# Unit-matrix products on TensorE for one operand turn and five weight parts, with a new order of head and tail

## The chip, the cores and the metric

The kernel runs on one core of a Trainium2 chip. The core has a matrix engine (TensorE, PE in the profile; its weight loads are PEld), a vector engine (VectorE, DVE), a scalar engine (ScalarE, ACT), a general engine (GpSimd, POOL) and SyncE (SP), whose queue issues nearly all transfers. The engines run their own instruction streams in order and wait for one another by semaphores. TensorE writes its results into banks of PSUM; DVE and ACT read them from there. The metric is the device time of one execution in microseconds; the median of five runs is used. All times are microseconds unless marked otherwise.

## The reference

There are 128 graphs of 128 nodes with 512 features (`x`, 128x128x512, float32) and a weighted adjacency (`adj`, 128x128x128). Two layers run one after the other for each graph:

```python
# layer 0
h = max(layernorm(x), 0)
H = (adj != 0); w = adj[:, 0, :]              # hyperedge weights: first row
S = H diag(1/colsum(H)) H^T;  Dinv = 1/(H w)
r = relu(Dinv * (S @ (h @ W1^T)) + b1)         # 512 -> 1024
r = layernorm(r) * gamma + beta
y = Dinv * (S @ (r @ W2^T)) + b2               # 1024 -> 512
x = x + (y + h)
# layer 1
h = max(layernorm(x), 0)
agg = (adj @ h) / max(rowsum(adj), eps)
x = x + relu([h, agg] @ W^T)                   # 1024 -> 512
```

Results are wanted in float32.

## The kernel before, in words

**Products in three parts.** A float32 product runs on TensorE in the faster format fp32r by splitting both operands into three parts: a high part `h` (ACT, a scaled copy), a low part `l` (DVE or POOL, the difference) and a third part `d` (DVE). `product` (L392 to L408) puts `h` by `h` and `l` by `l` into one PSUM bank (`rm`, `gm`, `bm`, `am` by the product's name; L401) and `d` by `d` into a second (`rd`, `gd`, `bd`, `ad`; L406). ACT and DVE then read both banks and add them up. Six banks serve these products in turn, two more the node products (`ps_s`, `pz`, `py`).

**The weights.** The three weight matrices w1, w2 and w3 are held as two halves each (class `Half`), each of four 128x512 blocks k. A half is split once, in the head: `high(i)` on ACT (L143), `low(i)` on DVE (L147) and `rest(i)` on DVE (L153), each for two blocks k at a time (i is 0 or 1). That makes twelve subtractions `l - h` at L153, which write the tile `d` over the raw weights.

**The graphs.** One graph passes through these stages, each a small function:
- norm of x, `incidence` and `node_matrix` (L303 to L325), `conv1_nodes` (`pz`, L359), the split of z (L372, L376, L379), the two halves of the product with w1 (`rm`, `rd`), `conv1_main` on ACT (L421), `conv1_out` on DVE (L426), `conv1_bias` (L431, through the helper at L80);
- sums and spread of the inner norm (L240, L245), `inner_norm` (L256), then a *round trip*: `inner_out` writes the result to a scratch tensor in memory (L447), `inner_in` reads it back in four blocks (L455), `inner_turn` turns 32x32 blocks on DVE (L462), so that the features lie over the partitions; the split into `nh`, `nl`, `nd` (L483, L80, L492); the product with w2 (`gm`, `gd`), `conv2_main` (L521), `conv2_weights_out` (L525), `conv2_bias`, `conv2_nodes` (`py`, L534), `conv2_out` (L538);
- layer 1: norm of the new x (L240, L245, L256), again a round trip (`layer1_trip_out`, `layer1_trip_in`, `layer1_turn`; scratch `h_scratch`, block tile `hb`, turned tile `ht`), the split into `hh`, `hl`, `hd`, the products with both halves of w3 (`layer1_mean`: `bm`, `bd`; `layer1_self`: `am`, `ad`), the evictions of the first (L585, L589), its split (`bh`, `bl`, `bd`), `aggregate` (L616) with the adjacency, `layer1_self_main` (L610), `layer1_self_out` (L622), `finish` (L627 and the store, L628);
- the adjacency for `aggregate`: `mean_operator` (L266 to L269) divides its rows by their sums on DVE, `mean_out` writes it to scratch, `mean_in` reads it back in four blocks (`anb`, L214), `mean_transpose` turns it on DVE (`ant`, L287) and splits off its high part on ACT (`anp`, L290), `mean_rest` makes the other two parts (L293, L294).

**The order.** The program is recorded in an order written out by hand, and each engine's stream is that order. `step(s)` (L633 to L698) interleaves stages of six neighbouring graphs; `head()` (L700) starts the pipeline and splits the weights between the first graphs' stages; `tail()` (L924) runs the last five graphs out, called a to e (123 to 127). A stage that has been done is not done again. `combine` (L75) adds two tiles, on POOL in pieces of 256 columns, on DVE in one instruction; `conv1_bias`, `conv2_bias` and the low parts take the engine as an argument and use POOL without one. `fill(n)` asks for a filler product of n columns ahead of the next bank's first user (L94): TensorE multiplies constants there.

Of the kernel before, what the change touches and what calls it, by code (L numbers as in the profile page):

```python
# [24 lines left out]
def gnn_kernel(  # L25
# [31 lines left out]
    nc = tc.nc  # L57
# [28 lines left out]
    def fill(columns, diff=False):  # L86
        (FILL_DIFF if diff else FILL).append(columns)
# [21 lines left out]
    def stage(f):  # L109

        def run(g, *a):
            key = f, g, *(v for v in a if type(v) is int)
            if 0 <= g < N and key not in done:
                done.add(key)
                f(g, *a)

        return run
# [14 lines left out]
    class Half:  # L132
# [16 lines left out]
        def rest(self, i, eng=nc.vector):  # L149
            if self.d is None:  # L150
                self.d = const.tile([P, KD, 512], FP, tag=self.name + "d", name=self.name + "d").bitcast(FR)
            c = slice(2 * i, 2 * i + 2)
            eng.tensor_tensor(self.d[:, c], self.l[:, c], self.h[:, c], SUB)  # L153

    w1, w2, w3 = ([Half(f"w{n}{i}") for i in range(2)] for n in (1, 2, 3))

# [27 lines left out]
    def load_affine():  # L184
        for j in range(Q):
            for i, v in enumerate((beta, gamma)):
                nc.gpsimd.dma_start(
                    out=gb[B * j : B * (j + 1), i].rearrange("a (l m) -> a l m", m=2),
                    in_=v.rearrange("(l a) (j m) -> j a l m", a=B, j=Q)[j])
# [323 lines left out]

    @stage
    def conv2_weights(g):
        PG[g] = product(N_LEFT.pop(g), w2, lambda pm: PY.update({g: pm}), "g")
# [183 lines left out]
    def head():  # L700
# [6 lines left out]
        load_affine()  # L707
        load_adjb(0, nc.scalar)
# [15 lines left out]
        fill(3072)  # L724
# [4 lines left out]
        w1[0].rest(0)  # L729
        conv1_high(0)  # L730
        w1[1].high(1)
        load_bias(b1_bc, b1)
# [5 lines left out]
        w1[0].rest(1)  # L738
# [4 lines left out]
        incidence(1)  # L743
        conv1_weights(0, 0)
# [5 lines left out]
        w1[1].low(0)  # L750
        scale_w2(1, nc.scalar)
        w1[1].rest(0)
        w1[1].rest(1)
# [8 lines left out]
        w2[0].high(0)  # L762
# [20 lines left out]
        inner_spread(0)  # L783
        scale_w2(4, nc.vector)
        scale_w2(5, nc.vector)
# [5 lines left out]
        incidence(2)  # L791
        inner_norm(0)
        fill(256)
# [39 lines left out]
        w2[1].rest(0)  # L833
# [3 lines left out]
        inner_rest(0)  # L837
        w3[0].high(1)
        load_adjb(5)
        w2[1].rest(1)  # L840
# [12 lines left out]
        fill(384)  # L853
# [4 lines left out]
        conv1_high(3, True)  # L858
        conv1_low(3)
        conv1_main(2, 1)  # L860
        conv1_rest(3)
        conv1_weights(3, 0)
        conv2_out(0)
# [14 lines left out]
        layer1_trip_out(0)  # L878
        conv1_bias(2, 1, nc.vector)
        mean_operator(0)  # L880
# [31 lines left out]
        mean_transpose(0)  # L912
        node_scale(4)
        inner_in(2)
        w3[0].rest(0)
# [4 lines left out]
        w3[1].rest(1)  # L920
        load_x(5)
        load_adjb(6)

    def tail():  # L924
        a, b, c, d, e = range(N - 5, N)
        layer1_self_main(a)
        conv2_bias(c)
        layer1_high(b)
        conv2_nodes(c)
        layer1_self_out(a)  # L930
        mean_out(b)
        inner_out(d)
        inner_in(d)
        finish(a)
        layer1_low(b)
        load_adj(c)
        mean_in(b)
        conv1_main(e, 0)
        conv2_out(c)
        conv1_weights(e, 1)  # L940
        layer1_sums(c)
        layer1_spread(c)
        layer1_rest(b)
        conv1_out(e, 0)
        conv1_main(e, 1)
        layer1_mean(b)
        inner_turn(d)
        scales(c, 3)
        layer1_self(b)
        conv1_out(e, 1)  # L950
        inner_high(d)
        conv1_bias(e, 0)
        layer1_norm(c)
        layer1_mean_main(b)
        mean_transpose(b)
        conv1_bias(e, 1)
        inner_low(d)
        layer1_mean_out(b)
        layer1_trip_out(c)
        inner_sums(e)  # L960
        layer1_mean_high(b)
        inner_spread(e)
        scales(e, 2)
        inner_rest(d)
        layer1_mean_low(b)
        conv2_weights(d)
        mean_operator(c)
        mean_rest(b)
        layer1_mean_rest(b)
        aggregate(b)  # L970
        inner_norm(e)
        conv2_main(d)
        layer1_trip_in(c)
        conv2_weights_out(d)
        layer1_turn(c)
        layer1_self_main(b)
        conv2_bias(d)
        layer1_high(c)
        fill(384)
        conv2_nodes(d)  # L980
        layer1_self_out(b)
        mean_out(c)
        inner_out(e)
        load_adj(d)
        inner_in(e)
        finish(b)
        layer1_low(c)
        mean_in(c)
        conv2_out(d)
        layer1_sums(d)  # L990
        layer1_rest(c)
        layer1_spread(d)
        layer1_mean(c)
        inner_turn(e)
        scales(d, 3)
        layer1_self(c)
        inner_high(e)
        layer1_norm(d)
        layer1_mean_main(c)
        mean_transpose(c)  # L1000
        layer1_mean_out(c)
        inner_low(e)
        layer1_trip_out(d)
        layer1_mean_high(c)
        mean_operator(d)
        inner_rest(e)
        layer1_mean_low(c, nc.vector)
        conv2_weights(e)
        mean_rest(c)
        layer1_mean_rest(c)  # L1010
        aggregate(c)
        conv2_main(e)
        layer1_trip_in(d)
        conv2_weights_out(e)
        layer1_turn(d)
        layer1_self_main(c)
        conv2_bias(e)
        layer1_high(d)
        fill(768)
        conv2_nodes(e)  # L1020
        layer1_self_out(c)
        layer1_low(d)
        mean_out(d)
        finish(c)
        mean_in(d)
        conv2_out(e)
        load_adj(e)
        layer1_sums(e)
        layer1_rest(d)
        layer1_mean(d)  # L1030
        layer1_spread(e)
        scales(e, 3)
        layer1_self(d)
        layer1_norm(e)
        layer1_mean_main(d)
        mean_transpose(d)
        layer1_mean_out(d)
        layer1_trip_out(e)
        layer1_mean_high(d)
        mean_operator(e)  # L1040
        layer1_mean_low(d, nc.vector)
        mean_rest(d)
        layer1_mean_rest(d)
        aggregate(d)
        layer1_trip_in(e)
        layer1_turn(e)
        layer1_self_main(d)
        layer1_high(e)
        layer1_self_out(d)
        mean_out(e)  # L1050
        layer1_low(e, nc.vector)
        mean_in(e)
        layer1_rest(e)
        fill(1536)
        layer1_mean(e)
        finish(d)
        layer1_self(e)
        layer1_mean_main(e)
        mean_transpose(e)
        layer1_mean_out(e)  # L1060
        layer1_mean_high(e)
        mean_rest(e)
        layer1_mean_low(e)
        layer1_mean_rest(e)
        aggregate(e)
        layer1_self_main(e)
        layer1_self_out(e)
        finish(e)
# [40 lines left out]
```

## Time and profile before

| What | us |
|---|---|
| median of 5 runs | 2504.09 (2503.63 to 2505.43) |
| time of the profiled execution | 2505.43 |
| its span, first to last instruction | 2503.6 |
| mean granted TensorE clock | 0.998 of full |
| first `aggregate` (graph 0) starts, by the chain | 101.38 |
| `aggregate` of graph 123 starts, by the timeline | 2443.14 |
| last matmul (`aggregate` of graph 127) starts | 2498.56 |
| last store issued on SP | 2500.59 |

The profile is one execution, taken by the hardware profiler. Its page gives the busy time of each engine, the span in 40 slices, and the chain of work that ended last, followed back from the end. Answers of the trace give the same in a window of time: busy times by stretch, the chain in order of time, and a timeline (start, duration, engine, line, operation, output and inputs, count; in brackets the idle time of the engine just before, and what ended it). A duration includes the latency until the result is written; queued instructions of an engine overlap by that latency, so that they follow one another at a shorter interval than they last. A float32 matmul appears as two records, an fp32r matmul as one.

### The profile page before, as it was taken

To read this page: it belongs to the slowest core of one execution; us is meant where nothing else is said; L and a number is where in the kernel's file an instruction comes from. 1 tells how busy PE (TensorE), PEld (TensorE's weight loads), DVE (VectorE), ACT (ScalarE), POOL (GpSimd) and SP (SyncE) were. 2 spreads that over 40 slices of the span, in tenths; PEclk is the share of its full clock that TensorE was granted. 3 is DMA by queue.
4 is the path that set the end of the run, shared out by engine and by line. 5 is a ranking of instruction groups with operands and counts; after the bars stand their busy time and mean duration, and the time that the engine had idled before them with its cause. 6 is when DMAs were issued, how large, how long until landed. Compare 5 with 4: busy or idle time off the path is not lost.

```text
span 2503.6 us, 41081 instructions
## 1 busy us (share of the span) xinstructions
PE 2476.2 (99%) x11196; PEld 2005.3 (80%) x11196; DVE 2003.6 (80%) x4910; ACT 1936.0 (77%) x4112; POOL 1715.6 (69%) x2284
## 2 busy tenths in 40 slices
PE   8899999999999999999999999999999999999998
PEld 5688888888888888888888888888888888888886
DVE  7888887878888788888877888887887888788785
ACT  6778778777877877887787788778778877877874
POOL 2477677677767767776776777677677767767773
PEclk9999999999999999999999999999999999999999
DMA  6343443444344344334434433443443344344332
GB/s 176 102 123 119 128 132 120 123 131 123 119 128 132 120 125 130 121 119 129 130 120 127 129 121 119 130 130 121 128 128 121 120 130 128 120 128 129 120 113 94
DMA packets 409671, 311.87 MB, mean 125 GB/s; under 512 B 176736, under 2 KB 340576, under 8 KB 409440
## 3 DMA queue, kind: packets, MB, share of 16 engines
q1 hardware_dynamic: 408608, 309.18, 40.0%
q8 instruction: 88, 1.44, 0.3%
q14 instruction: 143, 1.17, 0.2%
q10 hardware_dynamic: 576, 0.07, 0.0%
q0 software_dynamic: 256, 0.01, 0.0%
HBM read 166.47 MB, written 142.61 MB: 123 GB/s over the span
## 4 chain that ended last, share of the span: by engine, by line
PE 96%; DVE 2%; DMA 1%; ACT 1%; SPq 0%; issue 0%; POOL 0%; POOLq 0%; DVEq 0%; ACTq 0%
PE rm L401 18%; PE gm L401 18%; PE gd L406 9%; PE bm L401 9%; PE am L401 9%; PE rd L406 9%; PE bd L406 5%; PE ad L406 5%; PE pz L359 4%; PE py L534 4%; PE am L616 2%; PE ad L616 1%; PE ps_s L321 1%; DMA w11r<-in_w1t_dram 0%; DMA w20r<-in_w2t_dram 0%
## 5 line engine op out<-in xcount | busy, mean ns | idle before, releaser
L80 POOL TENSOR_TENSOR g<-g,c 128x256 f32<-128x256 f32 x252 | 181.7, 741 | 646.6 <-DVE g L525 646.6
L80 POOL TENSOR_TENSOR r<-r,b_bc 128x256 f32<-128x256 f32 x500 | 360.9, 743 | 53.2 <-DVE r L426 43.5
L80 POOL TENSOR_TENSOR nl<-nt,nh 128x256 fp32r<-128x256 f32 x504 | 357.8, 742 | 4.1 <-ACT nh L483 4.1
L80 POOL TENSOR_TENSOR x_t<-x_t,b_bc 128x256 f32<-128x256 f32 x256 | 242.1, 966 | 17.0 <-DMA b_bc<-in_b_dram 17.0
L240 ACT ACTIVATE h<-x_t 128x512 f32<-128x512 f32 x256 | 160.1, 625 | 105.9 <-DVE x_t L538 103.9
L610 ACT ACTIVATE o<-am 128x512 f32<-128x512 f32 x128 | 76.8, 600 | 213.5 <-PE am L616 213.5
L80 POOL TENSOR_TENSOR hl<-ht,hh 128x256 fp32r<-128x256 f32 x252 | 235.9, 957 | 2.7 <-ACT hh L483 2.7
L80 POOL TENSOR_TENSOR x_t<-x_t,h 128x256 f32<-128x256 f32 x256 | 181.2, 726 | 41.9 <-ACT h L256 41.9
L256 ACT ACTIVATE h<-x_t,st 128x512 f32<-128x512 f32 x256 | 205.9, 804 | 1.8 <-DVE st L252 1.7
L426 DVE SCALAR_TENSOR_TENSOR r<-rd,dinv,r 128x512 f32<-128x512 f32 x256 | 190.5, 744 | 17.8 <-PE rd L406 12.9
L589 DVE TENSOR_TENSOR gb_t<-bd,gb_t 128x512 f32<-128x512 f32 x128 | 88.6, 692 | 140.8 <-ACT gb_t L585 138.4
L538 DVE SCALAR_TENSOR_TENSOR x_t<-py,dinv,x_t 128x512 f32<-128x512 f32 x128 | 96.1, 750 | 123.1 <-PE py L534 123.1
L80 POOL TENSOR_TENSOR bl<-gb_t,bh 128x256 fp32r<-128x256 f32 x252 | 181.9, 745 | 15.5 <-PE am L401 15.5
L359 PEld LDWEIGHTS pz<-s,h 128*128 128x128 f32 x1024 | 134.2, 192 | 66.6 <-ACT s L323 46.8
L245 ACT ACTIVATE h<-x_t,st 128x512 f32<-128x512 f32 x256 | 183.8, 718 | 4.3
L421 ACT ACTIVATE r<-rm,dinv 128x512 f32<-128x512 f32 x256 | 173.2, 677 | 1.7 <-PE rm L401 1.7
L525 DVE TENSOR_TENSOR g<-gd,g 128x512 f32<-128x512 f32 x128 | 88.5, 692 | 96.5 <-PE gd L406 91.2
L462 DVE STREAM_TRANSPOSE nt<-nb 128x1024 f32<-128x1024 f32 x128 | 157.5, 1230 | 1.6 <-DMA nb<-n_scratch 1.0
L256 ACT ACTIVATE r<-r,st 128x1024 f32<-128x1024 f32 x128 | 157.7, 1232 | 1.3 <-DVE st L252 1.3
L492 DVE SCALAR_TENSOR_TENSOR nd<-nh,nl 128x1024 fp32r<-128x1024 f32 x128 | 155.9, 1218 | 0.0
L627 DVE SCALAR_TENSOR_TENSOR o<-o,x_t 128x512 f32<-128x512 f32 x128 | 150.9, 1179 | 4.3
L401 PE MATMUL rm<-w11h,z 128*128 128x512 f32 x512 | 151.4, 417 | 0.0
(138 smaller groups left out, 7215.2 us busy)
## 6 DMA issues: line engine op xcount, KB each, us to landing
n_scratch<-r SPq DMA_DIRECT2D x128, 512.0 KB, 2.7
nb<-n_scratch SPq DMA_DIRECT2D x512, 128.0 KB, 2.8
x_t<-in_x_dram SPq DMA_DIRECT2D x128, 256.0 KB, 3.0
h_scratch<-h SPq DMA_DIRECT2D x128, 256.0 KB, 2.0
hb<-h_scratch SPq DMA_DIRECT2D x512, 64.0 KB, 2.0
out_dram<-o SPq DMA_DIRECT2D x128, 256.0 KB, 2.2
adj_t<-in_adj_dram SPq DMA_DIRECT2D x128, 64.0 KB, 1.9
an_scratch<-adj_t SPq DMA_DIRECT2D x128, 64.0 KB, 1.7
```

What stands on the lines that cost most here:

```text
L80: eng.tensor_tensor(dst[:, s], a[:, s], b[:, s], op)
L240: copy(junk, src, func, accum_out=t[:, 0:1])
L245: copy(junk, src, AF.Square, bias=t[:, 1:2], accum_out=t[:, 2:3])
L256: copy(dst, src, func, bias=t[:, 5:6], scale=t[:, 4:5])
L359: nc.tensor.matmul(z[:, k * P : (k + 1) * P], H0[g][:, k * P : (k + 1) * P], S[g], start=True, stop=True)
L401: nc.tensor.matmul(pm, left[i](k), right(i, k), start=(i == 0 and k == 0), stop=(i == 1 and k == kk - 1))
L406: nc.tensor.matmul(pd, left[2](k), right(2, k), start=(k == 0), stop=(k == kk - 1), skip_group_check=True)
L421: copy(R[g][:, HALVES[half]], PY.pop((g, half)), AF.Copy, scale=DN[g][:, 1:2])
L426: nc.vector.scalar_tensor_tensor(r, PR.pop((g, half)), dn[:, 0:1], r, MUL, ADD)
L462: nc.vector.transpose(nt.rearrange("p k (i b) -> p k i b", b=B), t.rearrange("p i k a -> p k i a"))
L492: nc.vector.scalar_tensor_tensor(t, h, 2.0**-12, low, MUL, SUB)
L627: nc.vector.scalar_tensor_tensor(o, o, 0.0, X.pop(g), MAX, ADD)
```

## The change

`Half.rest` gets a second way. Called with an engine it does what it did. Called without, it makes the third part of each of its two blocks on TensorE: `l` times the unit matrix plus `h` times minus the unit matrix, in one bank, which ACT copies into `d`. Five of the twelve calls are made that way: both of the first half of w2, the second of the first half of w3, and both of the second half of w3. `unit()` makes the two matrices on POOL early in the head, in the space of the tiles `anp` and `ant`, which graph 0 needs later.

The last graph's layer 1 operand no longer takes the round trip. `layer1_norm_now` writes the normed tile with its columns in the order that the turned blocks have (ACT), `turned_now` turns it with four products by a unit matrix on TensorE into one bank, and ACT and DVE take the high and the low part from there; the third part is made as before. `turn_unit` makes that unit matrix on POOL in the tail. One write, four reads and one turn on DVE go.

Stages of head and tail change places, some additions and low parts of the tail move from POOL to DVE, and some fills change size. `step` is not changed.

```diff
-        def rest(self, i, eng=nc.vector):
+        def rest(self, i, eng=None):
+
             if self.d is None:
                 self.d = const.tile([P, KD, 512], FP, tag=self.name + "d", name=self.name + "d").bitcast(FR)
-            c = slice(2 * i, 2 * i + 2)
-            eng.tensor_tensor(self.d[:, c], self.l[:, c], self.h[:, c], SUB)
+            if eng:
+                c = slice(2 * i, 2 * i + 2)
+                eng.tensor_tensor(self.d[:, c], self.l[:, c], self.h[:, c], SUB)
+                return
+            for k in (2 * i, 2 * i + 1):
+                b = bank("wd")
+                nc.tensor.matmul(b, UNIT[0], self.l[:, k], start=True, stop=False)
+                nc.tensor.matmul(b, UNIT[1], self.h[:, k], start=False, stop=True)
+                copy(self.d[:, k], b, AF.Copy)
...
+    def turned_now(key, src, tags, stages):
+        done.update((v.f, key[1]) for v in stages)
+        k = src.shape[1] // P
+        h, l = (left.tile([P, k, P], FP, tag=tag, name=key[0] + m).bitcast(FR) for tag, m in zip(tags, "hl"))
+        for i in range(0, k, 4):
+            b = bank("pt")
+            for n in range(4):
+                nc.tensor.transpose(b[:, n * P : (n + 1) * P], src[:, (i + n) * P : (i + n + 1) * P], TURN[0])
+            t = b.rearrange("p (n c) -> p n c", n=4)
+            copy(h[:, i : i + 4], t, AF.Copy, scale=DOWN)
+            nc.vector.tensor_tensor(l[:, i : i + 4], t, h[:, i : i + 4], SUB)
+
+        def rest():
+            d = left.tile([P, k, P], FP, tag=tags[2], name=key[0] + "d").bitcast(FR)
+            nc.vector.scalar_tensor_tensor(d, h, 2.0**-12, l, MUL, SUB)
+            return [lambda n, v=v: v[:, n] for v in (h, l, d)]
+
+        return None, rest
...
     def head():
...
         load_affine()
+        unit()
...
-        fill(3072)
+        fill(2944)
...
+        w1[1].low(0)
         conv1_weights(0, 0)
...
+        w2[0].high(0)
         conv1_nodes(1)
...
+        scale_w2(5, nc.vector)
         scale_w2(4, nc.vector)
-        scale_w2(5, nc.vector)
...
+        load_adjb(5)
         w3[0].high(1)
-        load_adjb(5)
...
         conv2_weights_out(0)
-        fill(384)
         conv1_nodes(3)
         conv2_bias(0, nc.vector)
         fill(384)
         conv2_nodes(0)
         conv1_high(3, True)
+        fill(384)
         conv1_low(3)
...
+        mean_operator(0)
         conv1_bias(2, 1, nc.vector)
-        mean_operator(0)
...
-        mean_transpose(0)
         node_scale(4)
         inner_in(2)
-        w3[0].rest(0)
+        w3[0].rest(0, nc.vector)
         layer1_low(0, nc.vector)
         w3[0].rest(1)
         layer1_rest(0)
         w3[1].rest(0)
         w3[1].rest(1)
+        load_adjb(6)
         load_x(5)
-        load_adjb(6)
+        mean_transpose(0)
 
     def tail():
...
-        conv2_bias(c)
...
+        inner_out(d)
+        turn_unit()
         layer1_high(b)
+        conv2_bias(c, nc.vector)
...
+        layer1_low(b, nc.vector)
...
+        conv1_bias(e, 0, nc.vector)
...
+        conv1_bias(e, 1, nc.vector)
+        inner_low(d, nc.vector)
...
+        layer1_mean_low(b, nc.vector)
...
+        fill(512)
+        conv2_bias(d, nc.vector)
+        inner_out(e)
...
+        layer1_low(c, nc.vector)
...
+        fill(640)
...
+        layer1_norm_now(e)
         layer1_mean_low(d, nc.vector)
...
+        mean_operator(e)
...
+        layer1_now(e)
         layer1_self_out(d)
+        fill(1408)
...
+        layer1_mean_low(e, nc.vector)
         layer1_mean_rest(e)
         aggregate(e)
         layer1_self_main(e)
```

The tail's fills were 384, 768 and 1536 columns before. In `finish` of graph 125 and 124 the call moves behind the next graph's loads and sums.

## The prediction

> **What bounds the kernel now.** I read the page first, for who is busy and what chain ended last.
>
> ```profile
> PE 2476.2 (99%) x11196; PEld 2005.3 (80%) x11196; DVE 2003.6 (80%) x4910; ACT 1936.0 (77%) x4112; POOL 1715.6 (69%) x2284
> PE 96%; DVE 2%; DMA 1%; ACT 1%; SPq 0%; issue 0%; POOL 0%; POOLq 0%; DVEq 0%; ACTq 0%
> ```
>
> TensorE is busy nearly throughout. So I asked next for busy times by stretch; columns: span of the stretch, then busy time of PE, weight loads, DVE, ACT, POOL, granted clock, DMA share, GB/s.
>
> ```profile
> 38.00:98.00 60.00, 47.11 (x187) 31.61 (x188) 53.67 (x106) 41.91 (x81) 17.86 (x22) 1.00 0.28 85
> 98.00:101.40 3.40, 3.40 (x9) 2.66 (x9) 1.94 (x9) 1.28 (x4) 0.00 (x0) 0.52 0.65 231
> 101.40:2443.10 2341.70, 2341.70 (x10702) 1915.30 (x10702) 1885.99 (x4667) 1841.90 (x3930) 1665.59 (x2214) 1.00 0.40 125
> 2461.60:2503.60 42.00, 33.70 (x122) 21.84 (x120) 24.25 (x50) 15.58 (x32) 10.63 (x14) 0.97 0.25 79
> ```
>
> Between 101.4 and 2443.1 us (123 graphs of 19.04 us) TensorE never rests, and the step is not edited: that stage stays. In 38 to 98 us DVE is the fullest engine (53.7 of 60); just behind, TensorE runs 3.4 us at a clock of 0.52. After 2461.6 us it is a string of dependences. Only these ends can move. Third, the chain of waits in order of time, in the head (start, length, piece):
>
> ```profile
> 66.13 1.24 DVE nl L80
> 67.39 1.22 DVE nd L492
> 68.61 0.61 DVE r L80
> 69.25 1.16 ACT r L240 x2
> 70.67 1.25 ACT junk L245 x2
> 72.15 0.58 ACT g L521
> 72.72 1.19 ACT r L256
> 96.45 1.22 DVE nd L492
> 97.71 3.66 PE gd L406 x8
> 101.38 0.48 PE am L616 x2
> ```
>
> The head ends where `nd` of graph 2 lets `gd` start at 97.71; from there TensorE is dense. Last, the timeline of the tail:
>
> ```profile
> 2463.40 1.12 PE L534 MATMUL py<-g,s 128*128 128x512 f32 x2 [0.98 <-POOL g L80]
> 2491.36 1.20 PE L401 MATMUL bm<-w30h,hh 128*128 128x512 f32 x4 [0.85 <-ACT hh L483]
> 2496.36 1.42 POOL L80 TENSOR_TENSOR bl<-gb_t,bh 128x256 fp32r<-128x256 f32 x2 [15.48 <-PE am L401]
> 2498.56 0.50 PE L616 MATMUL ad<-bd,anp 128*128 128x512 f32 x1 [0.22 <-DVE bd L492]
> ```
>
> The last graph's `bm` waits for the round trip of its operand, and the last matmul for a slow `bl` on POOL.
>
> **Head: the third parts.** Five of the twelve L153 subtractions leave DVE (1.22 us each, one per 1.14 when queued). Each becomes four 128x512 matmuls and two ACT evictions. Four L401 matmuls take 0.91, so 0.23 each; a 128x512 eviction (`z`, L372) takes 0.60, one per 0.50 when queued. In all PE gets 20 x 0.23 = 4.6, ACT 10 x 0.50 = 5.0 to 6.0, DVE loses 5.7. The question is who is late at each place.
> - First pair of k (41 us): DVE loses the row at 41.14, but its next, `z`, waits for ACT's `z` (42.20 to 42.80), as before. Gain 0. The two evictions fit into ACT's 2.16 idle ahead of `nh` (45.91).
> - Second (48.4 us): its matmuls follow `rd`, so the evictions stand at 49.1 to 50.1, ahead of the sums of graph 1, which started at 49.54. Those slip 0.5; behind them wait DVE's reciprocal and `nd`, which stood 0.3 behind ACT's result. Cost +0.2 to 0.25 there; the 1.14 saved on DVE buys nothing.
> - `mean_operator(0)` (L266 to L269, 69.13 to 70.04, 0.9 us) is put ahead of the bias at 68.61. The chain shows bias, sums, spread, `g`, norm in a row: +0.9, uncovered. Together +1.15: DVE's turn of graph 0 (79.58) starts at 80.7, and the last low part of w3 ends at 82.4 instead of 81.3.
> - Three parts of w3: DVE then has four small ones 0.55, one third part 1.14, `hl` 0.6, `hd` 0.6, `ant` 0.25: done at 85.6, where before it was at 87.88. But ACT does `hh` and `s` to 82.1 and then six evictions. Four of TensorE's six large banks are held by graph 3 until ACT and DVE read them, so the pairs alternate on two: (0.50 + two matmuls with their drain 0.62 + two handovers 0.1)/2 = 0.6 each, 82.1 to 85.85. Then `anp`, `r` (L421) at 85.95, and by the same sequence as before (L421 at 81.85 to L372 at 85.03, now without the gap) `nh` at 89.65, before 89.81. POOL's second bias ends at 91.4 (92.3), the sums of graph 3 start at 91.8 (92.36), their square root ends at 95.2 (95.7), `nd` starts at 95.9 (96.45), `gd` at 97.15 (97.71). Gain 0.55.
> - TensorE: pairs to 85.3, `pz`, `bm` at 86.2, `am`, `ad` to 91.6, `gm` to 95.2 without a break, then 2.0 idle.
>
> **The clock.** The eight `gd` matmuls took 97.71 to 101.17, 3.46 us, at half clock; at the rate of later ones (1.82) that is 1.64 less. The Trainium skill ("TensorE: Matmul & The Clock Gate", Part 1: The HAM clock gate) has the clock halved after an idle window of about 3.4 us. Taken as a single gap this would have given no half clock here: the longest gap was 1.8. The trace says otherwise: in the 3.4 us before 97.9 only four matmuls ran (0.9 us, 27%). Yet 1.73 idle at 64.3 among dense work (about 47%) left the clock at 1.00. The new window holds 2.0 idle and 1.4 work, 41%, nearer the second. I take warm: gain 1.6, bounds 0 and 1.6. Head in sum: 2.2 earlier (bounds 0.5 late to 3.5 early).
>
> The rest of the head costs nothing: `w2[0].high(0)` moves on ACT ahead of `z` of graph 1 (+0.5), covered by DVE's 1.05 idle at 26.7 (without it, +0.5 on that path). The other moved lines leave DVE's and ACT's own order as it was, or swap two scalings whose inputs are both there; the fills stand where TensorE waits anyway; the five loads of x(5) and adjb(6) change places on an SP queue that is then free until 91.60. The unit matrices (memset, two selects on POOL) have no row; POOL idles 17 us until 26.06 and the first user comes at 41. Bounds 0 and 0.4 (an L153 beside POOL's adds took 1.64 for 1.22); I take 0. `mean_transpose(0)`, moved last, keeps the unit tile's space free and is needed 9 us later.
>
> **Tail, in the times of before.** DVE takes over biases and low parts from POOL.
> - Bias of `g` of graph 126: POOL 1.42 becomes 0.65 behind a 0.64 turn, so `py` at 63.2 (2463.40 before; I drop 2400). `hl` on DVE (0.65) instead of POOL (1.85). `bd` of graph 125 then waits for `hd` to 65.75, against 66.21. Gain 0.46. Earlier, `nd` of 126 moves behind `nl`, `bl` on DVE: 58.0 for 57.39, done at 59.1 where `gd` stood at 59.09: covered just; without cover up to 0.4.
> - Graph 127: `gd` at 73.03, POOL bias to 77.2, `py` at 77.25 (77.90). The turn of graph 126 still waits for its load, issued when `bl` frees the tile at 74.0: 77.65 (77.57). So `bm` of 126 starts at 79.0 as before; `hd` no longer waits behind L627, `bd` at 81.4 (81.66); `x_t` of 127 at 78.9 (79.50).
> - Operand of 127 before: norm, one write and four reads on SP (2.1 us of queue), landing, turn at 89.87, `hh` 90.68, `bm` 91.36. After: norm at 84.0 to 84.8 (behind `bh`), `aggregate` of 126 to 85.75 (was 87.65, its `bl`, `bd` wait less), four transposes, `o`, `hh` 86.5 to 87.1, `hl` 87.75, `hd` 89.0; `bm` at 87.6. Gain 3.7. The transposes have no row. Nearest: four fp32 128x128 products at L359, 0.89. The Trainium skill (same page, Part 4: PE-mode transpose) says 275 to 390 ns each and that they don't count as busy for the clock: 1.1 to 1.6. I take 0.9; the price of the rule makes `bm` 0.2 to 0.5 later, covered by what follows.
> - What is late next: TensorE would be done with `ad` at 93.0, but the turned adjacency of 127 is not. `mean_operator` ends at 86.3, its write is out at once (before it stood behind the reads, 88.18), four reads 88.1 to 89.9, in use 1.8 later (1.6 before, 91.70 to 93.28): `ant` 91.7, `anp` 92.1, `bh` 92.3 to 92.9, `bl` on DVE to 93.6 (POOL 1.42 before), `bd`, last matmul at 94.3, before 98.56. **Tail: 4.2 earlier** (bounds 2.0 and 5.5). What follows (L622, L627, 3.0 us of store) stays.
>
> **The sum.** The profiled execution took 2505.43 (span 2503.6 and 1.8 around it): 2505.43 - 2.2 - 4.2 = 2499.0. The median is 1.34 lower, so 2504.09 - 6.4 = 2497.7.
>
> **Rivals.**
> - *ACT takes DVE's place, and the clock drops all the same*: gd starts about as before and runs cold. Head 0 to 0.6; total -4.2 to -4.8: 2499.6. For it: ACT already paces `nh`, sums and `st`; two edits lengthen the path by 1.15. Against: the window above is fuller. Chance 0.26.
> - *Another wait binds the tail*: the norm's new output pattern, or DVE, now fullest, delays `bl`, and half of the 4.2 goes; with the head 2.2: -4.3: 2499.8. For it: DVE stands in every link. Against: it idles 2.5 and 2.24 there before. Chance 0.12.
> - *Slower: no overlap on the two banks at 82 us*. If each pair waits out its eviction with a cold clock (two matmuls 0.87, drain 0.2, eviction 0.60, handovers 0.1), a turn is 1.8, six are 10.6 for 3.7: `gd` +6.3 late, less 4.2: 2506.2. It decides for slower from 8.4 for six (1.4 each). Against: the clock stayed at 1.00 in 78 to 86 us before with less work. Chance 0.05; over 0.2% of it only with more.
> - *More*: DVE's 5.7 counts beyond the 0.55, -9: 2495. DVE is fullest; but each place showed ACT or a load behind it. Chance 0.07.
> - The likeliest, -6.4: 0.50, own range 2496 to 2499.5.
>
> **How the numbers follow.** 0.2% (about 5.0 us, what a measurement of this kernel can tell from no change) lies at 2499.1. The likeliest with nine tenths of its chance, the last rival and some of the first two lie below it: 0.60. Slower by over 0.2%: 0.04. Range 2494.5 to 2502.5, leaving out the slower case and the ends of the bounds.
>
> **What would show it.** Right: in the head `gd` of graph 2 at 97 us with eight matmuls in 1.8 us and clock 1.00; six evictions of about 0.6 at 82 to 86; sums of graph 2 at 70.4; `am` L616 at 99. In the tail no load of `hb` for graph 127; its `bm` within 2 us of the end of the aggregate of 126 (3.7 before); the last `bl` on DVE, with `anp` waiting for the load of the adjacency. Wrong: half clock still in the 3 us after `gd`; ACT waiting over 1 us per pair; the last `bm` still behind ACT by over 1 us.

## The result, and the profile after

The changed kernel takes 2497.95 us (median of 23 runs, 2496.88 to 2499.12) against 2503.98 for the kernel before (43 runs beside it): ratio 0.9976, interval 0.9971 to 0.9982. That is 0.25 from the forecast of 2497.7. The profiled execution took 2499.2, its span is 2497.4.

The sum was right, but its terms were not. I cut both spans at the same two places, the start of the first `aggregate` matmul of graph 0 and of graph 123:

| us | up to graph 0's `aggregate` | the 123 graphs (each) | from graph 123's to the end |
|---|---|---|---|
| before | 101.17 | 2341.81 (19.039) | 60.62 |
| changed | 99.38 | 2338.44 (19.012) | 59.59 |
| difference | -1.8 | -3.4 | -1.0 |
| forecast | -2.2 | 0 | -4.2 |

These starts are read from the timeline. The chain counts a piece from the end of the one before it, and so has 101.38 and 2443.14 for the same two matmuls of the kernel before; 2443.14, given above as the timeline's, is the chain's.

Lines have moved in the changed kernel: `product` is L422 and L427 (L401, L406 before), `aggregate` L677 (L616), `conv2_nodes` L595 (L534), the split L504 and L513 (L483, L492), the sums L261 and L266 (L240, L245); L160 to L162 are the new third parts, L542 to L545 the new turn. The page of the changed kernel, line of busy times:

```profile
PE 2473.8 (99%) x11220; PEld 2009.4 (80%) x11220; DVE 2005.3 (80%) x4913; ACT 1940.9 (78%) x4122; POOL 1701.8 (68%) x2269
```

There are 24 more matmul records than before, and yet 2.4 us less of TensorE's busy time: some matmuls have become shorter. Busy times by stretch, columns as before the change (span; PE, weight loads, DVE, ACT, POOL; granted clock, DMA share, GB/s):

```profile
38.00:98.00 60.00, 51.22 (x208) 36.29 (x207) 47.26 (x96) 46.17 (x90) 16.89 (x22) 0.97 0.27 79
98.00:101.40 3.40, 3.40 (x16) 2.81 (x15) 3.19 (x13) 1.92 (x6) 0.90 (x2) 1.00 0.61 221
99.40:2437.80 2338.40, 2338.40 (x10702) 1915.47 (x10701) 1889.20 (x4669) 1841.65 (x3930) 1667.34 (x2216) 1.00 0.40 125
```

In the head DVE lost 6.4 us and ACT took 4.3; behind it the clock is 1.00 where it was 0.52, and 16 matmul records fall into it where 9 did. The third row is the surprise: the same 10702 matmuls, back to back, took 2338.4 where they took 2341.7. The chain of the head, in order of time:

```profile
66.80 1.23 DVE nd L513
...
68.93 0.61 DVE r L80
69.56 1.16 ACT r L261 x2
...
85.74 0.60 ACT w31d L162
...
96.16 1.22 DVE nd L513
...
97.42 2.12 PE gd L427 x8
```

The division of the adjacency now stands between `nd` and the bias `r`; the last eviction of a third part, at 85.74, is itself a piece of the chain. `gd` starts only 0.29 earlier than before, but takes 2.12 and not 3.66. The tail, by the timeline (start, duration, engine, line, operation; in brackets the idle time ahead):

```profile
2473.96 1.13 PE L595 MATMUL py<-g,s 128*128 128x512 f32 x2 [0.55 <-POOL g L80]
2482.76 0.60 PE L542 MATMUL pt<-unit,h 128*128 128x128 f32 x4
2483.19 2.54 PE L94 MATMUL bm<-eps 128*128 128x512 f32 x6
2485.27 1.38 PE L422 MATMUL bm<-w30h,hh 128*128 128x512 f32 x4
2490.41 0.69 DVE L80 TENSOR_TENSOR bl<-gb_t,bh 128x512 fp32r<-128x512 f32 x1
2492.00 0.50 PE L677 MATMUL ad<-bd,anp 128*128 128x512 f32 x1 [0.33 <-DVE bd L513]
```

The round trip of the last operand is gone, `bl` is on DVE. But `py` of graph 127 starts 36.15 after graph 123's `aggregate`, before it was 34.92: something in the tail lost 1.2 where 0.65 was to be won.

### The profile page after: what moved, and what is told of

It is laid out like the page before. It is cut to its first block, busy times and chain, and to the rows that moved or that the text cites. A ratio compares the mean times of both kernels' runs of the same rounds, so it can differ in the third digit from the quotient of the medians.

```text
span 2497.4 us, 41112 instructions
## 1 busy us (share of the span) xinstructions
PE 2473.8 (99%) x11220; PEld 2009.4 (80%) x11220; DVE 2005.3 (80%) x4913; ACT 1940.9 (78%) x4122; POOL 1701.8 (68%) x2269
## 3 DMA queue, kind: packets, MB, share of 16 engines
q8 instruction: 88, 1.44, 0.2%
## 4 chain that ended last, share of the span: by engine, by line
PE 96%; ACT 1%; DVE 1%; DMA 1%; issue 0%; SPq 0%; POOL 0%; DVEq 0%; ACTq 0%
PE rm L422 18%; PE gm L422 18%; PE gd L427 9%; PE bm L422 9%; PE am L422 9%; PE rd L427 9%; PE bd L427 5%; PE ad L427 5%; PE pz L380 4%; PE py L595 4%; PE am L677 2%; PE ad L677 1%; PE ps_s L342 1%; DMA w11r<-in_w1t_dram 0%; DMA w20r<-in_w2t_dram 0%
## 5 line engine op out<-in xcount | busy, mean ns | idle before, releaser
L261 ACT ACTIVATE h<-x_t 128x512 f32<-128x512 f32 x256 | 160.0, 625 | 105.8 <-DVE x_t L599 102.9
L266 ACT ACTIVATE h<-x_t,st 128x512 f32<-128x512 f32 x256 | 183.7, 717 | 4.3
L483 DVE STREAM_TRANSPOSE nt<-nb 128x1024 f32<-128x1024 f32 x128 | 157.6, 1232 | 4.1 <-DMA nb<-n_scratch 3.9
L513 DVE SCALAR_TENSOR_TENSOR nd<-nh,nl 128x1024 fp32r<-128x1024 f32 x128 | 155.9, 1218 | 0.0
L422 PE MATMUL rm<-w11h,z 128*128 128x512 f32 x512 | 151.4, 417 | 0.0
```

The lines of the kernel that those rows point to most:

```text
L261: copy(junk, src, func, accum_out=t[:, 0:1])
L266: copy(junk, src, AF.Square, bias=t[:, 1:2], accum_out=t[:, 2:3])
L422: nc.tensor.matmul(pm, left[i](k), right(i, k), start=(i == 0 and k == 0), stop=(i == 1 and k == kk - 1))
L483: nc.vector.transpose(nt.rearrange("p k (i b) -> p k i b", b=B), t.rearrange("p i k a -> p k i a"))
L513: nc.vector.scalar_tensor_tensor(t, h, 2.0**-12, low, MUL, SUB)
```

## The experiments

Each run has a median beside runs of the kernel before on the same chip (2503.88 to 2504.09), and a profile of its own, cut as above. All times are us.

| run | median | change | head | each of 123 | tail | place of `anp` |
|---|---|---|---|---|---|---|
| before | 2503.98 | | 101.17 | 19.039 | 60.62 | 32 |
| changed | 2497.95 | -6.0 | 99.38 | 19.012 | 59.59 | 256 |
| e1_early_place | 2500.71 | -3.4 | 99.66 | 19.013 | 60.76 | 256 |
| e2_moved_32 | 2503.45 | -0.6 | 98.31 | 19.052 | 59.62 | 32 |
| e5_others_moved | 2503.92 | 0.0 | 98.22 | 19.058 | 59.31 | 128 |
| e6_anp_only | 2501.68 | -2.2 | 99.04 | 19.045 | 59.69 | 32 |
| e9_place_256 | 2498.00 | -6.0 | 98.28 | 19.012 | 59.48 | 256 |
| e10_place_64 | 2502.73 | -1.3 | 98.17 | 19.045 | 58.90 | 64 |
| e3_new_tail | 2500.92 | -3.2 | 98.94 | 19.045 | 57.30 | 32 |
| e4_new_head | 2500.64 | -3.5 | 98.66 | 19.012 | 61.39 | 256 |
| e8_old_head_place | 2497.33 | -6.6 | 99.59 | 19.015 | 57.24 | 256 |
| e7_fetch_moved | 2496.27 | -7.6 | 97.92 | 19.012 | 57.74 | 256 |
| e11_bias_first | 2495.67 | -8.3 | 96.83 | 19.013 | 57.76 | 256 |
| e12_w3_on_dve | 2501.28 | -2.7 | 101.43 | 19.021 | 57.23 | 256 |

"Place" is the largest power of two that divides the byte address of the tile within a partition, as the program lays it out. The mean over 123 graphs includes the first step, in which a clock still low cost 0.1 in the kernel before and in e1, 0.4 in e8, 0.7 in e3 and 1.2 in e12; in e6 and e11 waits in that step cost 0.6 and 0.1.

**Where the 3.4 us of the unedited stage come from.** Comparing the two traces matmul by matmul, all 87 of a step start at the same distances, except four: from the last `gd` through the three of `aggregate` the steps are 0.235, 0.233, 0.234, 0.231 before and 0.227 after. Their waits are the same, their operands too. What differs is an address: `unit()` is the first to ask for the tiles `anp` and `ant`, so these now lie ahead of tiles that they lay behind.

```diff
+        for tag, shape in (("anp", [P, 3, P]), ("ant", [P, P])):
+            nc.gpsimd.memset(pool.tile(shape, FP, tag=tag, name="first"), 0.0)
         load_adjb(0, nc.scalar)
```

> The kernel before, with one edit: in the head POOL clears the tiles anp and ant once, ahead of graph 0, so that they get the places that they have in the changed kernel (anp starts at a multiple of 64 bytes of a partition instead of an odd multiple of 32). No work of the graphs changes. Theory 1 (the 0.027 us per graph that the steady stage lost come from where anp, the stationary operand of the aggregate, lies): the three aggregate matmuls follow one another at 0.227 instead of 0.233, a graph takes 19.01, and the time falls by 3.3 to about 2500.7. Rival (the shorter step comes from something that the new head or tail sets up, not from the place of the tile): the step stays at 19.038 and the time within 0.4 of the kernel before. A third outcome, a different step with the time moving by less, would mean that the place counts only in part.

Measured 2500.71 (ratio 0.9986, 0.9979 to 0.9992) and 19.013: two clearings in the head of the kernel before bring the whole 3.4. The groups of matmuls by shape (busy us, mean ns of one), first before, then this run:

```profile
L616 PE MATMUL am<-bl,anp 128*128 128x512 f32 x122 | 48.4, 397 | 0.0
```

```profile
L616 PE MATMUL am<-bl,anp 128*128 128x512 f32 x122 | 47.5, 389 | 0.0
```

Which property of the place counts took five more runs. My first guess was a multiple of 64 bytes.

```diff
+        for tag, width, n in (("B", D, 1), ("st1", 8, 2), ("adj", P, 1), ("ht", P, 1), ("sb", P + 1, 1)):
+            for _ in range(n):
+                nc.gpsimd.memset(pool.tile([P, width], FP, tag=tag, name="place", bufs=n)[:, :1], 0.0)
         t = pool.tile([P, 3, P], FP, tag="anp", name="unit").bitcast(FR)
```

> The changed kernel, with one edit: five tiles get their places in the head ahead of the unit matrices, so that anp and ant start at an odd multiple of 32 bytes of a partition, as in the kernel before; all other tiles that TensorE reads keep their address modulo 64. POOL clears one column of each of the five (six small instructions more). Theory 1 (place of anp): a graph takes 19.038 again, the time rises by 3.3 over the changed kernel to about 2501.3. Rival (the step comes from the order of head and tail): 19.01 per graph and 2498.0.

The step got longer than before the change, 19.052, and the time is 2503.45, above both expectations. So more than the address modulo 64 counts.

> As the run with the moved places, but anp and ant start at a multiple of 64 bytes again, while the five other tiles (h0, the statistics, the adjacency, adjt, sb) keep the places that they had in that run. If the place of anp alone decides: a graph takes 19.007 again and the time is 2498.0, give or take 0.5. If it is one of the other tiles: 19.047 per graph as in that run, 2503. If both count, between.

(Edit: as above, a gap of 32 bytes ahead of `anp`, and one buffer less for the counter.) With `anp` at a multiple of 128 the step was the longest of all, 19.058. The guess of 64 has fallen.

```diff
+        nc.gpsimd.memset(pool.tile([P, 8], FP, tag="gap0", name="gap"), 0.0)
         t = pool.tile([P, 3, P], FP, tag="anp", name="unit").bitcast(FR)
+        nc.gpsimd.memset(pool.tile([P, 8], FP, tag="gap1", name="gap"), 0.0)
...
-        cnt = pool.tile([P, 1], FP, tag="cnt", name="cnt", bufs=2)
+        cnt = sb[:, P + 1 : P + 2]
```

> The changed kernel with anp and ant alone at odd multiples of 32 bytes (32 bytes off where they were; every tile after them is 64 bytes further or where it was; the small counter of incidence lies in a spare column of sb). If the place of anp modulo 64 decides: 19.03 to 19.05 per graph, 2501 to 2503. If it is another tile: 19.007 and 2498.0.

19.045: with `anp` and `ant` shifted by 32 and 64 bytes and the five others by at most 64 from where the changed kernel has them, the gain is gone. That points at `anp` but does not prove it: `sb`, one column wider, also changed the steps around `ps_s` and behind `pz` by some ns. In every run that had the short step until then `anp` lay at one and the same address, 210176, which is 821 times 256. The last pair tests the multiple itself (diff against the run with the five tiles):

```diff
-        for tag, width, n in (("B", D, 1), ("st1", 8, 2), ("adj", P, 1), ("ht", P, 1), ("sb", P + 1, 1)):
+        for tag, width, n in (("B", D, 1),):
```

> The changed kernel with h0 placed ahead of anp: anp starts 2048 bytes further, again at a multiple of 256 bytes of a partition, h0 where it lay in the kernel before. Nothing else moves. So far anp was at a multiple of 256 in every fast run, and at an odd multiple of 32 or 128 in every slow one. If a multiple of 256 is what counts: 19.007 per graph and about 2498. If it was that one address, or the place of h0: 19.03 or more and 2501 to 2503.

> As the run with the place at 256, but the two small statistics tiles ahead of anp too: anp starts 64 bytes further, at an odd multiple of 64; every other tile that TensorE reads lies as in that run. If a multiple of 256 counts: slow, 19.03 to 19.06 per graph, 2501 to 2504. If a multiple of 64 is enough: 19.007 and 2498.

(In the second, `("st1", 8, 2)` is kept too.) At 212224, a multiple of 256: 19.012 and 2498.00. At 212288, 64 bytes further: 19.045 and 2502.73. The same group in the two runs, in that order:

```profile
L680 PE MATMUL am<-bh,anp 128*128 128x512 f32 x122 | 47.5, 389 | 0.0
```

```profile
L680 PE MATMUL am<-bh,anp 128*128 128x512 f32 x122 | 48.6, 398 | 0.0
```

Between these two runs `anp` is the only tile that TensorE reads in the step and that has moved. What follows: of seven places, the two at a multiple of 256 bytes gave the short step, and the five others a step longer by 0.027 to 0.047. Why is not shown: the weight loads of `anp` are recorded at 187 to 188 ns before and after, and at the other places the matmuls of the next product slip by some ns too.

**Head and tail apart.** The changed kernel with the whole `head` of before (every `rest` on DVE, no unit matrices; the diff shows it in part), and then the changed kernel with the whole `tail` of before:

```diff
     def head():
...
-        unit()
...
-        w2[0].rest(1)
+        w2[0].rest(1, nc.vector)
...
-        mean_operator(0)
         conv1_bias(2, 1, nc.vector)
+        mean_operator(0)
...
```

> The head of before, all third parts on DVE and no unit matrices in it (so anp keeps its old place), with the tail of the changed kernel. The prediction put the tail at -4.2: 2499.8. The two profiles, aligned at the aggregate of graph 123, put it at -1.0 (4.55 less the 3.4 in which graph 126 and 127 lose again before bm): about 2503.0. Rival: the loss of 1.5 at py of graph 127 in the profile was an accident of one execution (a late landing of its operand), then -2.5: 2501.5.

> The head of the changed kernel with its unit matrices and its five third parts on TensorE (so anp has its new place), and the tail of before. By the prediction's sum -2.2 for the head and nothing between: 2501.8. By the profiles -1.8 for the head and -3.4 for the 123 graphs: 2498.8. Rival for the head: the 1.2 us that it gained before 40 us came from an earlier landing of the first weights in that one execution and not from the change; then -0.6 and -3.4: 2500.0.

The new tail alone brought 3.2 (ratio 0.9987, 0.998 to 0.9993), between the prediction's 4.2 and the 2.5 of the rival, and 57.30 us of tail against 59.59 in the changed kernel, although both run the same code there. The new head alone, with the place, brought 3.5, which is the place and next to nothing; its tail, which is the old one, took 61.39 and not 60.7. So the new head makes each tail slower. The third run puts the place of `anp` to the old head and the new tail, by the unit matrices that nobody then uses:

```diff
         load_affine()
+        unit()
         load_adjb(0, nc.scalar)
```

> The head of before with all twelve third parts on DVE, the unit matrices made but not used (so anp has its new place), and the tail of the changed kernel. If the three parts add up (place -3.4, tail -3.2 as measured with the old head, nothing from the head): 2497.5, no slower than the changed kernel. If the new head with its third parts on TensorE is worth the 2.2 of the prediction: 2500.2 by taking that from the changed kernel's 2498.0.

2497.33: 3.4 and 3.2 do add up, to 6.6. With not one third part on TensorE the kernel is no slower than the changed one (ratio to before 0.9973, 0.9962 to 0.9983, against 0.9976).

**What the new head does to the tail.** The transfers in 6 us of the tail of the changed kernel, from just before the write of graph 127's inner operand (40 slices of GB/s; queue, packets, MB, share; issue, size, us to landing):

```profile
GB/s 72 27 171 209 31 0 191 410 382 382 300 355 410 410 492 178 239 48 0 0 27 0 0 27 0 27 27 27 27 27 27 3 24 0 0 0 0 0 0 0
...
q8 instruction: 1, 0.02, 1.0%
...
n_scratch<-r SPq DMA_DIRECT2D x1, 512.0 KB, 5.1
```

The reader is to see the row of 27s: for 2 us the last packets of the write follow one another singly, each some 0.16 us long. I read that as one of the sixteen DMA engines going on alone when the others are done; the trace does not name the engine of a packet. In the same window one packet of 16 KB came on queue 8, the kind "instruction", and took 0.93 us (1.0% of 16 times 6 us); it starts 17.8 after graph 123's `aggregate` and ends at 18.7, where the single packets begin. The four reads of `nb` are issued when the write has landed, so they started 5.2 after it, with the old head 2.8. There the packet came at 24.3. The twenty matmuls of the third parts, with their weight loads, put 40 instructions more into TensorE's stream ahead of the tail. The theory: that stream is fetched in such packets, and a longer stream is fetched earlier.

```diff
-                w = min(columns, 512)
+                w = min(columns, 160 if len(done) < 14 else 512)
...
-        fill(2944)
+        fill(2720)
```

> The changed kernel, with the first filler product cut into 17 pieces of 160 columns instead of six of up to 512: eleven matmuls or 44 TensorE instructions more ahead of everything, in a stretch in which TensorE had 1.9 us to spare. Theory (the write of graph 127's inner operand landed 2.4 us late in the changed kernel because a fetch of 16 KB of TensorE's instructions held one of the 16 DMA engines for 0.93 us 1.9 us after the write was issued; in the run with the old head and the new tail that fetch comes 6.5 us later and the write lands in 2.7): 44 instructions at about 9 per us move the fetch some 5 us forward, to 13.0 after the start of graph 123's aggregate, the write lands in 2.7, the last product of nodes comes 1.5 earlier and the time falls by about 1 to 1.5, to 2496.7. Rival (the late landing has another cause): 2498.0 and the write again at 5 us.

```profile
GB/s 188 34 181 212 27 0 0 437 410 437 410 382 410 437 410 215 260 127 0 0 0 0 0 0 0 0 75 116 205 280 260 225 294 198 301 225 328 314 307 254
...
n_scratch<-r SPq DMA_DIRECT2D x1, 512.0 KB, 2.7
```

The packet came at 10.1 (I had said 13.0), the write landed in 2.7, `py` of graph 127 started at 34.50 and not 36.15, and the time fell by 1.7 to 2496.27. That only TensorE's stream was lengthened and that queue 8's packet moved shows whose instructions they are. The other profiles agree. In the six profiles in which the packet falls upon the write (the changed kernel, e2, e5, e6, e9, e10) it ends between 18.2 and 18.9, and the write lands 2.07 to 2.11 after that end in each; in the five with the new tail in which it comes at another time the write lands at 18.4. The Trainium skill ("Runtime: NRT & Kernel Launch", Instruction fetch mechanics) says that an engine's instructions are fetched in blocks of 16 KiB by a DMA queue of its own, at a cost that is "mostly hidden". By the page the packet would cost little or nothing here; the trace has 1.65 at `py`, paid not by TensorE's own stream but by the data transfer beside it.

**What the third parts and the order are worth in the head.** Both runs are compared with the run with the moved fetch. The division of the adjacency behind the bias again:

```diff
-        mean_operator(0)
         conv1_bias(2, 1, nc.vector)
+        mean_operator(0)
```

> The run with the moved fetch, and the division of graph 0's adjacency put behind the bias of graph 2 again, as before. The prediction charged 0.9 for its new place, uncovered up to the sums of graph 2; by it those sums start 0.9 earlier, and what is late next (the evictions of the third parts, which wait for w3's low parts) moves with them: about 2495.4 against 2496.3. Rival: the head's end is set by ACT's evictions and adds, which have their own pace, and the adjacency then comes later: no gain, 2496.3 or a little more.

`gd` of graph 2 at 94.88; measured from ACT's `z` of that graph (L393, at 40.40 here and 40.61 there) it is 0.89 earlier. 2495.67, ratio to before 0.9967 (0.9955 to 0.9979): the fastest kernel of the study. Against the run with the moved fetch the medians differ by 0.6 and the runs overlap, so the 0.89 is the trace's word. Its six runs (2494.64 to 2496.65) all lie below the 23 of the changed kernel.

```diff
-        w3[0].rest(1)
+        w3[0].rest(1, nc.vector)
         layer1_rest(0)
-        w3[1].rest(0)
-        w3[1].rest(1)
+        w3[1].rest(0, nc.vector)
+        w3[1].rest(1, nc.vector)
```

> The run with the moved fetch, but the three third parts of w3 stay on DVE (the two of w2 on TensorE). The first filler has six pieces more, so that TensorE's stream has as many instructions as in that run and the fetch stays where it is. By the prediction DVE is then done 2.3 later (87.88 for 85.6), nd of graph 2 comes 0.55 later and gd runs cold, 1.6 more: 2498.4. Rival: TensorE stays warm because of the filler's new places or the two parts of w2, then only 0.55 or nothing: 2496.3 to 2496.9, and by the evictions spared even less.

2501.28: 5.0 slower, where 2.2 was said. ACT shows why (here, then in the run with the moved fetch):

```profile
87.91 0.31 ACT L311 ACTIVATE anp<-ant 128x128 fp32r<-128x128 f32 x1 [7.01 <-DVE ant L308]
```

```profile
80.98 1.08 ACT L162 ACTIVATE w30d<-wd 128x512 fp32r<-128x512 f32 x2
82.39 1.09 ACT L162 ACTIVATE w31d<-wd 128x512 fp32r<-128x512 f32 x2 [0.33 <-PE wd L161]
83.81 1.08 ACT L162 ACTIVATE w31d<-wd 128x512 fp32r<-128x512 f32 x2 [0.34 <-PE wd L161]
```

In the new order the turn of graph 0's adjacency stands last on DVE, behind the third parts, and everything of ACT's behind `anp` waits for it: measured from `z`, `gd` came 3.3 later, where I had 0.55. The clock dropped behind it (0.51 in 101.4 to 104.0); from `gd` on, the first step included, that cost 1.6, as I had said. With the old order, in which that turn comes first, the same parts on DVE cost nothing of the kind (2497.33). So order and third parts belong together, and this run does not measure the parts alone.

## Why the prediction was right, and where it was wrong

**"That stage stays": wrong, by 3.4 us.** I argued from the step's code. `unit()` was charged for its time on POOL alone, though the change is told above as taking the space of `anp` and `ant`; I did not ask where that puts them. The place of one stationary operand is 0.027 of 19.04 us, 123 times.

**The tail's 4.2: mis-sized, and then taken back.** Undisturbed (old head, new tail) it is 3.3: the last matmul stands 3.75 earlier, less some 0.3 to 0.4 behind it. The last store is issued at the same distance and lands in 2.0, as before; the loss lies behind its landing, 1.34 to the end of the span where 1.04 was. Its cause was not looked into.
- Bias on DVE, charged at 0.46: `py` of graph 126 at 20.18 from 20.42, so 0.24. `py` of 127: 34.54 from 34.92, so 0.4, where I had 0.65.
- The operand of 127, charged at 3.7: `bm` at 45.1 from 48.4, 3.2. The transposes were cheaper than my 0.9 and than the 1.1 to 1.6 worked out from the Trainium skill ("TensorE: Matmul & The Clock Gate", Part 4: PE-mode transpose): four in 0.60, from the first start to the last result. The step that failed is "`bm` at 87.6", which in the times of before came at 88.1: ahead of `bm` stand 1408 columns of filler, which I left out. The run with the old head and the place, by the timeline and by the chain:

```profile
2481.80 0.60 ACT L544 ACTIVATE hh<-pt 128x512 fp32r<-128x512 f32 x1 [0.72 <-PE pt L542]
2483.62 1.38 PE L422 MATMUL bm<-w30h,hh 128*128 128x512 f32 x4
```

```profile
2481.27 0.44 PE pt L542 x4
2481.71 2.37 PE bm L94 x6
2484.08 1.83 PE bm L422 x8
...
2490.32 0.51 PE ad L677
```

`hh` is done at 2482.40, 0.2 sooner than I had it, and `bm` starts 1.2 later, behind the filler. TensorE goes from the transposes to the end with one gap, for `bd`. Whether less filler would be faster was not tried. "What is late next", the turned adjacency, is there at the same moment: `ant` at 49.1 where I had 48.7, the last `bl` done at 51.0, TensorE's `ad` at 51.1. So the last matmul stands at 51.9 where I had 51.3.
- Not in my list: the fetch of instructions. In the changed kernel it cost 1.65 at `py` of 127 and 2.3 from `bm` of 126 to the end (59.59 for 57.24). In the run with the moved fetch another packet, 1.44 us at 45.7, fell among the reads of `anb`, of which one took 1.9 to issue; its last matmul stands at 52.35, not 51.86.

**The head's 2.2: 1.6 right, 0.55 mis-sized.** I measure from ACT's `z` of graph 2 (L372 before, L393 after) because everything ahead of it moves with the landing of the weights (the first product with w2, which waits for its load, started at 20.84 in the profile of before, at 19.39 in that of the changed kernel, and at 19.54 in one more of the old head): it stood at 42.20 in the profile of before, at 40.66 to 41.01 in three other runs of that head, and at 40.40 to 41.66 with the new one. So 1.2 of the 1.8 that the two profiles show in the head is not the change.
- *The clock, 1.6*: right. From `gd` to graph 0's `aggregate` it is 3.5 to 3.6 with the old head in four profiles, counting what the low clock adds in the first step, and 1.94 to 1.97 with the new one in all nine that keep the third parts on TensorE. Two rows, 98 to 101.4 us, of the old head and of the new one, both with the new tail and the place:

```profile
98.00:101.40 3.40, 3.40 (x12) 2.66 (x11) 1.98 (x7) 0.69 (x2) 0.74 (x2) 0.63 0.47 180
```

```profile
98.00:101.40 3.40, 3.40 (x17) 2.82 (x16) 2.73 (x8) 1.64 (x3) 1.76 (x3) 1.00 0.40 158
```

The ground given for it fits as well. The gap ahead of `gd` hardly changed (1.79 to 1.80 with the old head, 1.63 to 1.75 with the new one, where I had 2.0). What changed is the stretch ahead of it: the sixteen `gm` matmuls, the second half of which followed POOL's pieces of `nl` one by one, started over 4.6 us and now start over 3.4. The last four, before and in the run with the moved fetch:

```profile
94.48 1.44 PE L401 MATMUL gm<-w21l,nl 128*128 128x512 f32 x4
```

```profile
93.21 1.09 PE L422 MATMUL gm<-w21l,nl 128*128 128x512 f32 x4
```

That fits a clock that follows the share of work and not a single gap. No run changed that share alone, so the rule is not shown.

- *`gd` earlier by 0.55*: it is about 0.1 (55.46 to 55.51 after `z` with the old head, 55.37 to 55.42 with the new one where the clock held, order as in the changed kernel). The step that failed is the second pair of third parts, "cost +0.2 to 0.25 there": the sums of graph 1 slipped by 0.87, where I had 0.5, and the next `nd` by 0.60. DVE covered 0.27 of it, as I had, but the slip was larger. `mean_operator`'s 0.9 is right (0.89). The six evictions took 3.9, from the first start to the last end, where I had 3.75.
- *The clock in 78 to 86*, which I took as safe against the slower rival: in the changed kernel's own profile it fell to 0.57 in 82 to 86, the six evictions took 5.0, and `gd` came 56.41 after `z`. Such cold pairs cost 1.0, not the 6 of that rival, since evictions and matmuls did overlap. The eight other profiles with these evictions show 1.00 in that window. But two of the four with the old head (e3, e8) show 0.82 there: the 1.00 of the kernel before, on which I relied, was that of one execution.

**The rivals.** "ACT takes DVE's place" was true of the 0.55, its cold clock was not. "Another wait binds the tail" came true in size, 2.3, by none of the causes I had named. "Slower" came only as that 1.0, and "more" not at all.

**The sum by the runs**: place -3.4, new tail -3.2, head -1.7 (0.1 and the clock's 1.6), the fetch in the tail +2.3: -6.0, as measured. Mine was -6.4. A gain of 3.4 that I had not seen met a loss of 2.3 that I had not seen, and 1.0 and 0.5 too much charged to tail and head: that the total came out is luck.

## What to carry to other kernels

When a change allocates anything, compare the addresses of the operands in the hot loop before and after: a stage whose code is untouched can still move. Cut the spans of both profiles at the same events and compare each stage with its own forecast, since a right total proves no term; and take where a load landed from several profiles, not from one. Adding instructions to one engine moves its fetches, so a late landing that no queue explains is worth a look at the instruction packets.

## What the runs showed of the hardware that I had not expected

- With the stationary operand `anp` at an address that is no multiple of 256 bytes, the three matmuls followed one another at 0.229 to 0.241 us instead of 0.227.
- One fetch of 16 KB, 0.93 us long, made a write of 512 KB land in 5.1 instead of 2.7, and the write landed 2.07 to 2.11 after the fetch ended, in six profiles.
- In every kernel the group `rm<-w11h,z`, behind the node products, takes 414 to 416 ns, where `rm<-w10h,z` takes 389 at the short step; and in all but e6 every fourth graph is 0.02 longer. The tile `s` has four buffers, of which one lies at a multiple of 256. In e6 they lie at the same four addresses, and with `sb` one column wider no fourth graph is longer, so that place alone is not the cause. It stays open.
- The clock fell to 0.57 in 82 to 86 us in one profile of nine with nearly the same instructions there; what decides was not found.
